# A chunked sigmoid recurrence: shorter warm-up, a different interleaving of four streams, and one operand added on TensorE for some steps

## The chip, the cores and the metric

The kernel runs on one core of one Trainium2 chip. The metric is the device time of one execution in microseconds, of which the median over the runs is taken. A separately profiled execution gives the trace that all views here are read from.

## The reference, cut to what matters

The input is 32 images of 128 channels and 64 x 64 pixels. Layer 0 adds a group norm followed by a dynamic 3 x 3 convolution. Layer 1 treats the 4096 pixels of an image as tokens of 128 channels and adds a windowed attention, and then this recurrence over the tokens, which is all that the change touches:

```python
Wx = jnp.einsum('bti,hi->bth', x, W)
flat = Wx.reshape(B * T, H)
mean = jnp.mean(flat, axis=0)
var = jnp.var(flat, axis=0)
Wx = ((flat - mean) * jax.lax.rsqrt(var + BN_EPS) * gamma + beta).reshape(B, T, H)
Vt = V.T

def step(yt, wx_t):
    yt = jax.nn.sigmoid(wx_t + yt @ Vt)
    return (yt, yt)
y0 = jnp.zeros((B, H), dtype=Wx.dtype)
_, ys = jax.lax.scan(step, y0, jnp.swapaxes(Wx, 0, 1))
```

Here B = 32 images, T = 4096 tokens, H = 128 channels. V is the orthogonal factor of a QR decomposition. The ys are added to the tokens. All data are float32.

## The kernel before

The first 4018 us work through the images: convolution, attention and the product with W. They leave the tokens plus attention in the output in HBM, and the raw products z in the HBM tensor `z_d`, one image after the other. The tile `frames` in SBUF, which the images use for their input, is filled with z of the first two images towards the end. Two vectors per channel, `scl` and `shf`, fold the batch norm, so that a step computes sigmoid(scl z + shf + V y).

Then `by_runs` does the recurrence. It cuts the 4096 tokens of an image into 128 chunks (`NRUN`) of 32 (`RUN`) and runs all chunks side by side, as columns of one matrix. A chunk doesn't know the state that enters it, so it starts `WARM` tokens earlier, in the chunk before, from a rough state; the map contracts, and after the warm-up the state is close enough. The first chunk starts from zero and stays out of the warm-up (127 of 128 columns). A bound on V computed at the start of the kernel (`okv`, the largest row sum of the absolute values of a product of V with itself) chooses between `by_runs` and `by_steps`, which walks over the 4096 tokens one after the other.

Two images form a group (`NI` = 2), so a step works on 128 partitions x 256 columns, and there are 16 groups. A step has four operations, one on each engine, and each waits for the one before:

- TensorE: the product of `fVT` with the state `yw` into a PSUM tile `v` (L1926 in the warm-up, L1932 after it). A float32 product is two MATMUL records in the trace.
- VectorE: v = scl z + v, with z read from the group's tile with a step of 32 floats (L1927, L1933).
- ScalarE: the state yw = sigmoid(v + shf) (L1928, L1936). The first step of a group has no product, and ScalarE reads z itself (L1923).
- GpSimd: outside the warm-up, the state is copied over z in the tile (L1937).

Two buffers of `yw` and two of `v` alternate in each stream. When a group is through, GpSimd issues two DMAs that add its tile onto the output in HBM (L1940; here called the hand-over of the group). Then `load` (L1903, on SP's queue) fetches group g + 6 into the tile that has come free, so it has to wait for those DMAs. There are five tiles `zr` and `frames`: six groups in SBUF.

Four streams (`NSTR`) overlap their chains: stream j does groups j, j + 4, j + 8 and j + 12. They are Python generators. The loop under `live` takes a step of each stream in turn, and lets a further one in every 13 steps (`lag`), until all four run. The schedule is manual: instructions stand in each engine's queue in the order in which the Python code emits them, and each engine works through its queue in that order.

Of the kernel before, what the change touches and what calls it, by code (L numbers as in the profile page):

```python
# [8 lines left out]
F32 = mybir.dt.float32  # L9
AF = mybir.ActivationFunctionType  # L10
ALU = mybir.AluOpType
AX = mybir.AxisListType

P = 128
# [17 lines left out]
NQ = 8  # L32
UNIT = 256
RUN = 32
WARM = 20
NRUN = T // RUN
NI = 2
NSTR = 4
# [20 lines left out]
class Clock:  # L59
# [88 lines left out]
    def take(self, eng, pool):  # L148
        t = min(pool, key=lambda t: self.after(eng, t, True))
        pool.remove(t)  # L150
        return t
# [106 lines left out]
def hybrid_kernel(  # L258
# [24 lines left out]
    nc = tc.nc  # L283
# [4 lines left out]
    of = out.rearrange("b c h w -> c b (h w)")  # L288
# [107 lines left out]
    with tc.tile_pool(name="sb2", bufs=1) as sb2, tc.tile_pool(  # L396
        name="ps2", bufs=1, space=bass.MemoryType.PSUM
    ) as ps2:
        vv = ps2.tile([P, P], F32, name="vv")
        nc.tensor.matmul(vv, fVT, fVT, start=True, stop=True)  # L400
        va_ = sb2.tile([P, P], F32, name="va_")
        nc.scalar.activation(va_, vv, AF.Abs)
        vr = sb2.tile([P, 1], F32, name="vr")
        nc.vector.tensor_reduce(vr, va_, axis=AX.X, op=ALU.add)
        vt_ = ps2.tile([P, P], F32, name="vt_")
        nc.tensor.transpose(vt_, vr.to_broadcast([P, P]), ident)
        vm = sb2.tile([P, 1], F32, name="vm")
        nc.vector.tensor_reduce(vm, vt_, axis=AX.X, op=ALU.max)
        nc.vector.tensor_scalar(vm, vm, 1.2, None, ALU.is_le)
        nc.vector.tensor_copy(okv, vm)  # L410
    contr = nc.values_load(okv[0:1, 0:1], min_val=0, max_val=1)

# [1470 lines left out]
    def by_runs():  # L1883
# [3 lines left out]
        with ExitStack() as pb:  # L1887
# [8 lines left out]
            def load(g):  # L1896
                if g < NG:
                    if g % (NSTR + 2):
                        zs[g] = zp.tile([P, NI, NRUN, RUN], F32, name="zr")
                    else:  # L1900
                        zs[g] = framed.rearrange("p i (c r) -> p i c r", r=RUN)
                    for i in range(NI if g else 0):
                        nc.sync.dma_start(  # L1903
                            zs[g][:, i].rearrange("p c r -> p (c r)"), z_d[g * NI + i]
                        )
# [1 line left out]
            for g in range(NSTR + 2):  # L1907
                load(g)

            def stream(j):  # L1910
                yw = []
                for i in range(2):
                    yw.append(hp.tile([P, NI, NRUN], F32, name=f"yw{j}_{i}"))
                    nc.vector.memset(yw[i], 0.0)
                for g in range(j, NG, NSTR):
                    zt = zs[g]
                    if g >= NSTR:
                        for i in range(2):
                            nc.vector.memset(yw[i][:, :, 0:1], 0.0)
                    for r in range(RUN - WARM, RUN):  # L1920
                        y, z = yw[r % 2][:, :, 1:], zt[:, :, 0 : NRUN - 1, r]
                        if r == RUN - WARM:
                            nc.scalar.activation(y, z, AF.Sigmoid, bias=shf, scale=scl)  # L1923
                        else:
                            ps = p_v.tile([P, NI, NRUN], F32, name=f"v{j}")[:, :, 1:]
                            nc.tensor.matmul(ps, fVT, yw[1 - r % 2][:, :, 1:], start=True, stop=True)  # L1926
                            nc.vector.scalar_tensor_tensor(ps, z, scl, ps, ALU.mult, ALU.add)  # L1927
                            nc.scalar.activation(y, ps, AF.Sigmoid, bias=shf)  # L1928
                        yield
                    for r in range(RUN):  # L1930
                        ps = p_v.tile([P, NI, NRUN], F32, name=f"v{j}")
                        nc.tensor.matmul(ps, fVT, yw[1 - r % 2], start=True, stop=True)  # L1932
                        nc.vector.scalar_tensor_tensor(  # L1933
                            ps, zt[:, :, :, r], scl, ps, ALU.mult, ALU.add
                        )
                        nc.scalar.activation(yw[r % 2], ps, AF.Sigmoid, bias=shf)  # L1936
                        nc.gpsimd.tensor_copy(zt[:, :, :, r], yw[r % 2])  # L1937
                        yield
                    for i in range(NI):
                        nc.gpsimd.dma_start(  # L1940
                            of[:, g * NI + i],
                            zt[:, i].rearrange("p c r -> p (c r)"),
                            accum_op=ALU.add,
                            max_dma_last_dim=8192,
                        )
                    load(g + NSTR + 2)

            live = [stream(j) for j in range(NSTR)]
            step = 0
            lag = (WARM + RUN) // NSTR  # L1950
            while live:
                for st in list(live[: 1 + step // lag] if step < lag * NSTR else live):
                    try:
                        next(st)
                    except StopIteration:
                        live.remove(st)
                step += 1

    def by_steps():

# [108 lines left out]
```

## Time and profile before

| what | value |
|---|---|
| median of 3 runs | 4610.49 us (4604.08 to 4615.4) |
| profiled execution, its own time | 4604.75 us |
| its span | 4602.9 us |
| VectorE busy in the whole span | 3577.4 us (78%) |
| first sigmoid of the recurrence | 4020.07 us |
| hand-over of group 0, 12, 15 | 4135.80, 4488.86, 4577.82 us |
| VectorE instructions L1927 and L1933 in the recurrence | 816 |
| ScalarE, first step of a group (L1923) | 0.815 us each |
| ScalarE, other steps (L1936) | 0.473 us each |
| GpSimd, copy (L1937) | 0.686 us mean, 0.629 median |

The span is the time from the first to the last event of the profiled execution; the execution's own time lies 1.85 us above it. Instructions of the recurrence carry their own line numbers, while those of the images nearly all have L242, since a helper records them. In the timeline, a group such as "MATMUL ... x2" is one product. What stands in brackets behind an instruction is the idle time of its engine before it, and what ended it. A DMA share above 1 means that the engines' packet times overlap a little: the 16 DMA engines are full.

### The profile page before, as it was taken

To read this page: it belongs to the slowest core of one execution; us is meant where nothing else is said; L and a number is where in the kernel's file an instruction comes from. 1 tells how busy PE (TensorE), PEld (TensorE's weight loads), DVE (VectorE), ACT (ScalarE), POOL (GpSimd) and SP (SyncE) were. 2 spreads that over 40 slices of the span, in tenths; PEclk is the share of its full clock that TensorE was granted. 3 is DMA by queue.
4 is the path that set the end of the run, shared out by engine and by line. 5 is a ranking of instruction groups with operands and counts; after the bars stand their busy time and mean duration, and the time that the engine had idled before them with its cause. 6 is when DMAs were issued, how large, how long until landed. Compare 5 with 4: busy or idle time off the path is not lost.

```text
span 4602.9 us, 102351 instructions
## 1 busy us (share of the span) xinstructions
PE 4175.5 (91%) x41527; PEld 2065.4 (45%) x41527; DVE 3577.4 (78%) x5421; ACT 2492.7 (54%) x4012; POOL 1650.6 (36%) x1652
## 2 busy tenths in 40 slices
PE   5999999899899999999999999999999987379995
PEld 2444444444444444444444444444444444135552
DVE  7778878787787787788687787888778754479994
ACT  1455555455555555555545555555555555258883
POOL 3333333333333333334232332333333321037764
PEclk9999999999999999999999999999999999689996
DMA  3435555454554555564555455555555454439997
GB/s 99 129 117 168 180 160 184 153 175 152 172 179 154 177 178 167 168 196 157 168 177 171 161 185 156 170 169 168 164 185 163 152 197 146 169 156 249 286 261 147
DMA packets 467575, 789.38 MB, mean 171 GB/s; under 512 B 338048, under 2 KB 348304, under 8 KB 434320
## 3 DMA queue, kind: packets, MB, share of 16 engines
q1 hardware_dynamic: 456480, 715.38, 47.1%
q0 software_dynamic: 8704, 67.11, 7.1%
q8 instruction: 332, 5.44, 0.5%
q14 instruction: 155, 1.27, 0.1%
q10 hardware_dynamic: 1904, 0.18, 0.0%
HBM read 499.06 MB, written 276.76 MB: 169 GB/s over the span
## 4 chain that ended last, share of the span: by engine, by line
PE 60%; DVE 20%; DMA 9%; ACT 4%; issue 4%; POOL 2%; SPq 1%; ACTq 0%; DVEq 0%; POOLq 0%
PE nm L242 35%; PE sc L242 14%; PE av L242 10%; DVE zt L242 4%; DVE v L1933 4%; DMA place<-r_d 3%; DVE v L1927 2%; ACT ex L242 2%; DVE frames L242 2%; DMA out_dram<-zr 2%; DVE u L242 1%; PE v L1932 1%; SPq L242 1%; DMA zr<-z_d 1%; DVE cp L242 1%
## 5 line engine op out<-in xcount | busy, mean ns | idle before, releaser
L242 ACT ACTIVATE ex<-sc 128x1152 f32<-128x1152 f32 x896 | 1012.5, 1130 | 838.7 <-PE sc L242 802.5
L242 POOL TENSOR_TENSOR qe<-qs,mqk 128x576 f32<-128x576 f32 x448 | 609.4, 1363 | 746.4 <-PE sc L242 741.0
L242 PE MATMUL nm<-u,w 128*128 128x512 f32 x1536 | 800.4, 633 | 15.9 <-POOL w L242 14.8
L242 PE MATMUL sc<-qe,ks 32*128 32x288 f32 x7168 | 698.7, 459 | 105.0 <-ACT ext L242 41.9
L242 PE MATMUL av<-ex,VE 128*32 128x144 f32 x14336 | 631.2, 294 | 21.5 <-DVE avs L242 21.3
L242 PEld LDWEIGHTS sc<-qe,ks 32*128 32x128 f32 x7168 | 285.6, 185 | 621.1 <-issue 181.5
L242 PEld LDWEIGHTS av<-ex,VE 128*32 128x32 f32 x14336 | 371.5, 110 | 350.0 <-issue 255.8
L242 POOL TENSOR_TENSOR u<-frames 128x528 f32<-128x528 f32 x256 | 380.3, 1493 | 186.8 <-PE nm L242 184.3
L242 PE MATMUL nm<-u,h 128*128 128x512 f32 x768 | 396.9, 625 | 3.6 <-DVE frames L242 3.6
L242 PEld LDWEIGHTS nm<-u,w 128*128 128x128 f32 x1536 | 258.6, 192 | 287.4 <-issue 257.0
L1932 PE MATMUL v<-yw,fVT 128*128 128x256 f32 x1024 | 323.7, 439 | 44.8 <-ACT yw L1936 43.7
L242 ACT ACTIVATE place<-zt 128x1024 f32<-128x1024 f32 x256 | 262.7, 1052 | 82.7 <-DVE zt L242 62.1
L1937 POOL COPY zr<-yw 128x256 f32<-128x256 f32 x416 | 257.2, 686 | 125.6 <-ACT yw L1936 125.6
L1936 ACT ACTIVATE yw<-v,shf 128x256 f32<-128x256 f32 x512 | 241.2, 473 | 107.6 <-DVE v L1933 71.4
L242 PE MATMUL nm<-zt,fWc 128*128 128x512 f32 x512 | 290.7, 665 | 6.9 <-ACT zt L242 6.9
L1933 DVE SCALAR_TENSOR_TENSOR v<-zr,scl,v 128x256 f32<-128x256 f32 x416 | 257.9, 668 | 42.0 <-PE v L1932 42.0
L242 DVE SCALAR_TENSOR_TENSOR u<-u,u 128x528 f32<-128x528 f32 x256 | 244.3, 967 | 46.4 <-POOL u L242 44.9
L242 ACT COPY zt<-nm 128x512 f32<-128x512 f32 x256 | 149.5, 585 | 206.7 <-PE nm L242 204.0
L242 PE MATMUL nm<-place,avg 128*32 128x256 f32 x3072 | 239.8, 394 | 13.0 <-ACT place L242 12.8
L1926 PE MATMUL v<-yw,fVT 128*128 128x254 f32 x608 | 206.0, 436 | 46.8 <-ACT yw L1923 27.6
L1932 PEld LDWEIGHTS v<-yw,fVT 128*128 128x128 f32 x1024 | 158.9, 193 | 195.7 <-ACT yw L1936 189.5
L242 DVE SCALAR_TENSOR_TENSOR zt<-sc,gbk,zt 128x576 f32<-128x576 f32 (+1 forms) x192 | 175.0, 912 | 74.1 <-PE sc L242 73.0
(204 smaller groups left out, 6595.0 us busy)
## 6 DMA issues: line engine op xcount, KB each, us to landing
place<-r_d SPq DMA_DIRECT2D x384, 512.0 KB
place<-in_conv_k_dram SPq DMA_DIRECT2D x128, 576.0 KB
x_d<-frames SPq DMA_DIRECT2D x32, 2112.0 KB
place<-x_d SPq DMA_DIRECT2D x128, 528.0 KB
frames<-in_x_dram SPq DMA_DIRECT2D x128, 512.0 KB
out_dram<-zt SPq DMA_DIRECT2D x64, 1024.0 KB
z_d<-zt SPq DMA_DIRECT2D x64, 1024.0 KB
zr<-z_d SPq DMA_DIRECT2D x26, 2048.0 KB
```

The source lines that it names most:

```text
L242: got = f(*args, **kw)
L1926: nc.tensor.matmul(ps, fVT, yw[1 - r % 2][:, :, 1:], start=True, stop=True)
L1927: nc.vector.scalar_tensor_tensor(ps, z, scl, ps, ALU.mult, ALU.add)
L1932: nc.tensor.matmul(ps, fVT, yw[1 - r % 2], start=True, stop=True)
L1933: nc.vector.scalar_tensor_tensor(ps, zt[:, :, :, r], scl, ps, ALU.mult, ALU.add)
L1936: nc.scalar.activation(yw[r % 2], ps, AF.Sigmoid, bias=shf)
L1937: nc.gpsimd.tensor_copy(zt[:, :, :, r], yw[r % 2])
```

## The change

There are three parts.

- `WARM` goes from 20 to 16, and the bound that chooses `by_runs` from 1.2 to 1.02.
- The round-robin of the generators is replaced by a list scheduler in Python. `Stream` holds where a stream stands (group `g`, step `k`, engine `phase`), `take` keeps for each engine when it will be free by assumed costs, and the loop emits the instruction that can start first. The product of step k of group g is given an earliest time, 90 + 26 (g - 4 left / 48), with `left` the steps still to do. This is an order and not a wait: nothing holds an instruction back on the chip but its operands and its queue.
- A step may be done without VectorE. `inject` emits ahead of the step's own product a product of the diagonal matrix `dg` = diag(scl) with z into the same PSUM tile, and the own product is accumulated onto it (`start=not whole`). ScalarE then reads the sum. This is allowed for group 0, and for other groups where at most two streams are left; the scheduler decides at which steps. `dg` is computed once by VectorE (L1911 of the changed kernel).

The emitted order has 752 products with `fVT`, 58 diagonal products (32 in group 0, 7 in group 14, 19 in group 15), 694 VectorE instructions, 768 sigmoids and 512 copies.

```diff
 NQ = 8
 UNIT = 256
 RUN = 32
-WARM = 20
+WARM = 16
 NRUN = T // RUN
 NI = 2
 NSTR = 4
@@ -406,7 +406,7 @@
         nc.tensor.transpose(vt_, vr.to_broadcast([P, P]), ident)
         vm = sb2.tile([P, 1], F32, name="vm")
         nc.vector.tensor_reduce(vm, vt_, axis=AX.X, op=ALU.max)
-        nc.vector.tensor_scalar(vm, vm, 1.2, None, ALU.is_le)
+        nc.vector.tensor_scalar(vm, vm, 1.02, None, ALU.is_le)
         nc.vector.tensor_copy(okv, vm)
     contr = nc.values_load(okv[0:1, 0:1], min_val=0, max_val=1)
 
@@ -1907,54 +1907,127 @@
             for g in range(NSTR + 2):
                 load(g)
 
-            def stream(j):
-                yw = []
-                for i in range(2):
-                    yw.append(hp.tile([P, NI, NRUN], F32, name=f"yw{j}_{i}"))
-                    nc.vector.memset(yw[i], 0.0)
-                for g in range(j, NG, NSTR):
-                    zt = zs[g]
-                    if g >= NSTR:
-                        for i in range(2):
-                            nc.vector.memset(yw[i][:, :, 0:1], 0.0)
-                    for r in range(RUN - WARM, RUN):
-                        y, z = yw[r % 2][:, :, 1:], zt[:, :, 0 : NRUN - 1, r]
-                        if r == RUN - WARM:
-                            nc.scalar.activation(y, z, AF.Sigmoid, bias=shf, scale=scl)
+            dg = hp.tile([P, P], F32, name="dg")
+            nc.vector.tensor_scalar_mul(dg, ident, scl)
+            DIAG, PE, DVE, ACT, POOL, LAT = 0.9, 0.43, 0.56, 0.46, 0.64, 0.2
+            free = {"PE": 0.0, "DVE": 0.0, "ACT": 0.0, "POOL": 0.0}
+
+            def take(eng, at, cost):
+                at = max(at, free[eng])
+                free[eng] = at + cost
+                return at + cost
+
+            class Stream:
+
+                def __init__(self, j):
+                    self.j, self.g, self.k, self.phase = j, j, 0, "ACT"
+                    self.at = 10.0 * j
+                    self.ahead = self.ps = None
+                    self.read, self.kept = [-9.0, -9.0], [-9.0, -9.0]
+                    self.yw = []
+                    for i in range(2):
+                        self.yw.append(hp.tile([P, NI, NRUN], F32, name=f"yw{j}_{i}"))
+                        nc.vector.memset(self.yw[i], 0.0)
+
+                def step(self, k):
+                    warm = k < WARM
+                    c = slice(1, NRUN) if warm else slice(0, NRUN)
+                    r = RUN - WARM + k if warm else k - WARM
+                    z = zs[self.g][:, :, 0 : NRUN - 1, r] if warm else zs[self.g][:, :, :, r]
+                    return c, r, z
+
+                def start(self):
+
+                    at = max(self.at, free[self.phase])
+                    if self.phase == "PE":
+                        left = WARM + RUN - self.k
+                        at = max(at, 90.0 + 26.0 * (self.g - left * NSTR / (WARM + RUN)))
+                    return at
+
+                def due(self):
+
+                    if self.phase == "PE":
+                        return self.start()
+                    if self.phase == "DVE":
+                        return max(self.at, free["DVE"]) + DVE + ACT + 2 * LAT
+                    return max(self.at, free["ACT"]) + ACT + LAT
+
+                def inject(self):
+
+                    k = self.k if self.phase == "PE" else self.k + 1
+                    c, r, z = self.step(k)
+                    self.ahead = p_v.tile([P, NI, NRUN], F32, name=f"v{self.j}")
+                    nc.tensor.matmul(self.ahead[:, :, c], dg, z, start=True, stop=False)
+                    take("PE", self.read[k % 2] + LAT, DIAG)
+
+                def go(self):
+
+                    k = self.k
+                    c, r, z = self.step(k)
+                    y = self.yw[r % 2]
+                    if self.phase == "PE":
+                        whole = self.ahead is not None
+                        self.ps = self.ahead if whole else p_v.tile([P, NI, NRUN], F32, name=f"v{self.j}")
+                        self.ahead = None
+                        nc.tensor.matmul(self.ps[:, :, c], fVT, self.yw[1 - r % 2][:, :, c], start=not whole, stop=True)
+                        self.at = take("PE", self.at, PE) + 0.38
+                        self.phase = "ACT" if whole else "DVE"
+                        return
+                    if self.phase == "DVE":
+                        v = self.ps[:, :, c]
+                        nc.vector.scalar_tensor_tensor(v, z, scl, v, ALU.mult, ALU.add)
+                        self.at = take("DVE", self.at, DVE) + 0.25
+                        self.phase = "ACT"
+                        return
+                    if k:
+                        nc.scalar.activation(y[:, :, c], self.ps[:, :, c], AF.Sigmoid, bias=shf)
+                    else:
+                        nc.scalar.activation(y[:, :, c], z, AF.Sigmoid, bias=shf, scale=scl)
+                    end = take("ACT", max(self.at, self.kept[k % 2] + LAT), ACT)
+                    self.read[k % 2] = end
+                    if k >= WARM:
+                        nc.gpsimd.tensor_copy(z, y)
+                        self.kept[k % 2] = take("POOL", end + LAT, POOL)
+                    self.at, self.phase, self.k = end + LAT, "PE", k + 1
+                    if self.k == WARM + RUN:
+                        g = self.g
+                        for i in range(NI):
+                            nc.gpsimd.dma_start(
+                                of[:, g * NI + i],
+                                zs[g][:, i].rearrange("p c r -> p (c r)"),
+                                accum_op=ALU.add,
+                                max_dma_last_dim=8192,
+                            )
+                        load(g + NSTR + 2)
+                        self.g, self.k, self.phase = g + NSTR, 0, "ACT"
+                        if self.g < NG:
+                            for i in range(2):
+                                nc.vector.memset(self.yw[i][:, :, 0:1], 0.0)
                         else:
-                            ps = p_v.tile([P, NI, NRUN], F32, name=f"v{j}")[:, :, 1:]
-                            nc.tensor.matmul(ps, fVT, yw[1 - r % 2][:, :, 1:], start=True, stop=True)
-                            nc.vector.scalar_tensor_tensor(ps, z, scl, ps, ALU.mult, ALU.add)
-                            nc.scalar.activation(y, ps, AF.Sigmoid, bias=shf)
-                        yield
-                    for r in range(RUN):
-                        ps = p_v.tile([P, NI, NRUN], F32, name=f"v{j}")
-                        nc.tensor.matmul(ps, fVT, yw[1 - r % 2], start=True, stop=True)
-                        nc.vector.scalar_tensor_tensor(
-                            ps, zt[:, :, :, r], scl, ps, ALU.mult, ALU.add
-                        )
-                        nc.scalar.activation(yw[r % 2], ps, AF.Sigmoid, bias=shf)
-                        nc.gpsimd.tensor_copy(zt[:, :, :, r], yw[r % 2])
-                        yield
-                    for i in range(NI):
-                        nc.gpsimd.dma_start(
-                            of[:, g * NI + i],
-                            zt[:, i].rearrange("p c r -> p (c r)"),
-                            accum_op=ALU.add,
-                            max_dma_last_dim=8192,
-                        )
-                    load(g + NSTR + 2)
-
-            live = [stream(j) for j in range(NSTR)]
-            step = 0
-            lag = (WARM + RUN) // NSTR
+                            live.remove(self)
+
+            live = [Stream(j) for j in range(min(NSTR, NG))]
             while live:
-                for st in list(live[: 1 + step // lag] if step < lag * NSTR else live):
-                    try:
-                        next(st)
-                    except StopIteration:
-                        live.remove(st)
-                step += 1
+                best = None
+                for st in list(live):
+                    at = st.start()
+                    if best is None or (at, st.g) < best[0]:
+                        best = (at, st.g), st, False
+                    k = st.k if st.phase == "PE" else st.k + 1
+                    if st.ahead is not None or k >= WARM + RUN or (st.g and len(live) > 2):
+                        continue
+                    at = max(free["PE"], st.read[k % 2] + LAT, st.at if st.k == 0 else 0.0)
+                    if st.phase != "PE" and at + DIAG > st.due():
+                        continue
+                    if any(o is not st and at + DIAG > o.due() + 0.1 for o in live):
+                        continue
+                    if (at, st.g) < best[0]:
+                        best = (at, st.g), st, True
+                _, st, ahead = best
+                if ahead:
+                    st.inject()
+                else:
+                    st.go()
 
     def by_steps():
 
```

## Prediction

> **What bounds the kernel now.** The stage tables come first, because the page averages two very different programs: the images, to about 4018 us, and the recurrence, which alone is changed. I cut its last 580 us where the number of live streams changes. After the stretch and its length come busy us (and counts) of PE, PEld, DVE, ACT, POOL, then the clock of TensorE, the DMA share and GB/s.
>
> ```profile
> 4022.00:4052.00 30.00, 14.72 (x25) 6.01 (x24) 7.94 (x13) 5.66 (x12) 0.00 (x0) 0.50 1.01 428
> ...
> 4200.00:4230.00 30.00, 29.48 (x106) 15.83 (x106) 29.83 (x55) 25.33 (x54) 21.35 (x35) 1.00 0.97 230
> ...
> 4440.00:4470.00 30.00, 29.27 (x106) 15.92 (x106) 29.65 (x55) 25.32 (x54) 21.64 (x37) 1.00 1.02 278
> ...
> 4530.00:4560.00 30.00, 17.73 (x37) 8.18 (x36) 11.55 (x18) 8.52 (x18) 13.94 (x21) 0.61 0.74 150
> 4560.00:4603.00 43.00, 7.75 (x14) 2.99 (x12) 4.53 (x7) 3.31 (x7) 6.74 (x9) 0.50 0.64 130
> ```
>
> There are three regimes. With one stream (first and last rows) nothing is busy, TensorE has half its clock, and a step is pure latency. With four streams VectorE is full, and so, from 4200 on, are the DMA engines. Next, the timeline gives one stream's chain at full clock:
>
> ```profile
> 4068.15 0.70 PE L1932 MATMUL v<-yw,fVT 128*128 128x256 f32 x2 [0.64 <-ACT yw L1936]
> ...
> 4068.89 0.66 DVE L1933 SCALAR_TENSOR_TENSOR v<-frames,scl,v 128x256 f32<-128x256 f32 x1 [0.69 <-PE v L1932]
> ...
> 4069.59 0.47 ACT L1936 ACTIVATE yw<-v,shf 128x256 f32<-128x256 f32 x1 [0.88 <-DVE v L1933]
> ...
> 4070.11 0.70 PE L1932 MATMUL v<-yw,fVT 128*128 128x256 f32 x2 [0.65 <-ACT yw L1936]
> ```
>
> From product to eviction 0.74, to sigmoid 0.70, to the next product 0.52: 1.96 us a step. Alone, at half clock, it is 2.53 (4569.32 to 4571.85). The chain of waits in order of time says what ends last when all streams run:
>
> ```profile
> 4123.91 1.76 DVE v L1933 x3
> ...
> 4253.12 35.16 DMA out_dram<-zr
> 4288.77 24.66 DMA zr<-z_d
> ...
> 4331.51 1.69 DVE v L1933 x3
> ```
>
> Three evictions in 1.69, so 0.563 each and 2.25 for a round of four; and twice the chain runs through a group's hand-over (write, then the load into its place). The waits of the DMA queues and of the engines in this stage:
>
> ```profile
> SPq L1903 <- DMA out_dram<-zr: 230.2, 8, 32.4
> ...
> ACT yw L1923 <- DMA zr<-z_d: 2.8, 3, 1.5
> ```
>
> Loads always wait for a write, yet cost the engines only 2.8 us: the DMA is full, but just in time. Hand-overs in the timeline come 29.4 us apart (4135.8 for group 0 to 4488.9 for group 12: 353.1 for twelve), as do the DMA's completions (a write issued to its queue at 4370.69, the following load at 4406.35, the one after at 4435.78). So two limits coincide at 29.4.
>
> **What the Trainium skill says.** "TensorE: Matmul & The Clock Gate", Part 1, has half clock when idle and full clock after about 3.4 us of sustained work; the trace agrees in kind (0.50 with one stream, 1.00 with four), though products became short only 7.4 us after the second stream began (4053.0 to 4060.4). The same page, "Architectural detail", says ScalarE's queue is strict first-in, first-out: a sigmoid that waits for a load holds up all streams. "SBUF — State Buffer", "Door 1: The DMA port swizzle", says that reads pay when each access crosses a 16-byte line; the new product reads every 32nd float. ScalarE shows such a price (0.815 us at L1923, reading z, against 0.473 reading PSUM); no TensorE row does. "DMA: Bandwidth & Descriptors", "SWDGE vs HWDGE vs iDMA", says that a DMA engine takes the two kinds of queue in turn. The trace agrees: a load of 4.2 MB beside a write takes 24.66, against some 9.9 alone (the ten first DMAs, 21 MB in about 49 us).
>
> **The change, part by part.**
>
> *Fewer steps.* 4 warm-up steps less in 16 groups: 64 products, evictions and sigmoids. 64 x 0.563 = 36 us of VectorE, on the path wherever four streams run. The bound 1.02 only chooses the branch: V is orthogonal, so the row sums of |V V^T| should lie close to 1, and the same branch runs. Cost nil.
>
> *Diagonal products.* The order of instructions has 58 (32 in group 0, 26 in groups 14 and 15), so 694 evictions are left of 816. Each takes the 0.66 us eviction off its stream's chain (0.74 + 0.52 = 1.26 left) and puts d on TensorE. Ordinary products queued behind each other start 0.43 apart (two passes, 0.215 each, in the trace). Low end d = 0.43, if stride is free; high end two passes of 256 at ScalarE's strided 0.815/256, 1.6. VectorE's 0.563 per 256 strided elements gives two passes of 0.5; the diff's own scheduler has 0.9. I take d = 1.0. A lone step is then 0.43 + 1.0 = 1.43, and TensorE is full, so the clock should come up.
>
> *Start.* The order gives group 0 ten lone steps, 12 rounds with group 1, 12 with 1 and 2 (11 with a diagonal product), 13 with all. Lone: first sigmoid 0.9, 7.4 us cold (3.4 steps at about 2.2), 6.6 x 1.43: 17.7. Two streams: the other stream's chain, 2.0 x 12 = 24.0 (TensorE needs 1.86). Three: 3 x 0.43 + 1.0 = 2.29, x 11, and one of 2.02: 27.2. Four: 13 x 2.25 = 29.3. Last eviction to hand-over 2. Sum 100.2. The first sigmoid moves by 0.3 (dg, on VectorE's queue ahead of the memsets; the 2.2 us of memsets, all issued at once, lie ahead of no eviction for ten steps) to 4020.4. **First hand-over 4120.6**, against 4135.8. Groups 1 to 3 need their loads, which landed by 4029.7, 4039.5 and 4049.3; their first sigmoids come at about 4032, 4042 and 4053, so no wait, but little slack.
>
> *Four streams.* From hand-over 0 to 12 the order has 564 evictions: x 0.563 = 317.5 us, against 353.1: 26.5 a group. That is what VectorE wants; the DMA gives a group per 29.4. Count from hand-over 0. Its write lands at about 28 (with half of the next load beside it, as at 4164.4), the next at 52 without the idle gap of before, then one per 29.4; each load lands 25 after the write before it. Loads of groups 7 to 15 land at 77, 106, 136, 165, 195, 224, 253, 283, 312. The order wants them after 221, 279, 319, 365, 409, 467, 507, 553 and 597 evictions less the 91 made: 73, 106, 128, 154, 179, 212, 234, 260, 285. The wait of each first sigmoid stops all streams, so delays add: 4, 0, 4, 3, 5, 0, 4, 3, 5, **27 us of new waiting** on loads at the first sigmoid of a group. So group 15 starts at 312 and hand-over 12 comes at 345. The VectorE time saved here is mostly given back to the DMA. GpSimd's and SP's queues keep their content: 512 copies of about 0.63 and 16 hand-overs of 2.44 to issue, as before, and 26 loads in the same order, so I count nothing for them; GpSimd has 21 of 30 us filled.
>
> *End.* Three streams: 10.5 rounds x 2.02 (4506.01 to 4508.04) = 21.2. Two with diagonal products: three rounds hold 6 products and 4 diagonal ones, 6.58, so 11.5 x 2.19 = 25.2, against 28.9 for 13 rounds at a sinking clock. Lone: 11 x 1.43 + 1.5 = 17.2 against 33.3. Hand-over 15 at 408.6. Its write took 25.1 to the end of the span (4577.82 to 4602.9), and here the write of group 14 (issued 391.5, landing about 413) is still ahead of it: 413 + 20 + 3 = 436. **End 4120.6 + 436 = 4556.6, 46.3 less than the span of 4602.9.** That execution took 4604.75, the median of the three shown is 4610.49; 4610.49 x 4556.6 / 4602.9 = 4564.
>
> **Rivals.** *Loads in time.* If the loads slip in without a wait and d = 0.43, the start is 95 us, hand-over 15 comes at 374, and the bare DMA sum ends it: 10 x 29.4 + 6 x 20 + 4 = 418 after 4115.4, so 4533, or 4541 as a median. For it: before, the waits were 2.8 us. Against: a DMA share of 1.02 leaves no reserve.
>
> *The diagonal product is dear.* Everything counts d twice: at d = 1.6 start 117.5 and hand-over 15 at 424.6, end 4588 (4596). At 2.0 start 130, hand-over 15 at 435, end 4611. Break-even is near 1.9; at 2.4 the kernel is **slower**, about 4642. It needs over four times an ordinary product, past the high end above; the half clock holding on would be the way there.
>
> *It does something else.* If the tight bound failed, `by_steps` would run 4096 dependent steps; at an estimated 0.6 us (sigmoid and product shorter than the 1.26 above) 2460 us in place of 580.
>
> **How the numbers follow.** Loads bind, d about 1: 0.64, 4564. Loads in time: 0.17, 4541. d of 1.3 to 1.75, still faster: 0.10, about 4585. d near 1.9, within 0.3%, about what a measurement here can tell from no change: 0.03. Slower by d: 0.05; by the branch: 0.01. Hence 0.91, 0.03, 0.06. The range goes from the DMA floor with 3 us to spare, 4538, to d = 1.6, 4596.
>
> **What would show it.** Right: hand-over 0 near 4121; waits of the first sigmoid on loads of some 25 us in place of 2.8; VectorE below 9.5 tenths in the four-stream stretches; hand-overs 29.4 apart still; clock 1.00 to the last step; diagonal products starting about 1.0 ahead of the next product. Wrong: hand-overs 26.5 apart and no load waits (then the DMA had reserve), a lone step over 2 us (d or the clock), or a write of group 15 that starts at once.

## The result, and the profile after

The changed kernel takes **4564.54 us** (median; 4559.51 to 4565.91), the kernel before took 4610.49 us on the same chip. The ratio is **0.9899 [0.9885, 0.9914]**: 46 us or 1.0% faster. The forecast was 4564. The sum came out right although some of its terms did not; the ledger shows where they cancel. All stages are counted from the first sigmoid, since the end of the images stage, which neither kernel changes, wanders by some 10 us either way between executions (4013 to 4034 us in the profiles below).

| stage, us | before | predicted | after |
|---|---|---|---|
| first sigmoid | 4020.07 | 4020.4 | 4022.85 |
| from there to hand-over 0 | 115.7 | 100.2 | 95.3 |
| hand-over 0 to 12 | 353.1 | 345 | 357.3 |
| gaps 12 to 13, 14, 15 | 26.8, 28.8, 33.3 | 21.2, 25.2, 17.2 | 20.9, 22.5, 16.5 |
| hand-over 15 to the end of the span | 25.1 | 27.4 | 28.9 |
| span | 4602.9 | 4556.6 | 4564.1 |

The span fell by 38.8: the start gave 20.4, the last three gaps gave 29.2; the middle **cost** 4.2 although it has four steps less in every group, the tail cost 3.8, and the images ended 2.8 later. (The profiled execution took 4565.91.)

The stage table of the kernel after answers to the one of before. The columns are the stretch and its length, then busy us (and counts) of PE, PEld, DVE, ACT, POOL, the clock of TensorE, the DMA share and GB/s.

```profile
4024.00:4054.00 30.00, 29.37 (x86) 16.96 (x87) 5.24 (x8) 13.98 (x28) 1.14 (x2) 0.90 1.00 427
4118.00:4142.00 24.00, 23.61 (x83) 12.19 (x83) 23.32 (x45) 20.18 (x43) 20.00 (x33) 1.00 0.95 214
4142.00:4168.00 26.00, 25.52 (x91) 13.39 (x91) 25.32 (x48) 22.02 (x47) 18.64 (x31) 1.00 1.03 266
4194.00:4234.00 40.00, 34.72 (x117) 19.73 (x116) 33.66 (x61) 28.67 (x60) 25.33 (x42) 0.91 0.97 260
4284.00:4318.00 34.00, 26.80 (x89) 15.56 (x88) 25.54 (x47) 21.33 (x45) 20.41 (x33) 0.85 1.03 288
4496.00:4519.00 23.00, 23.00 (x77) 14.84 (x77) 4.59 (x7) 10.92 (x23) 16.12 (x27) 1.00 0.97 195
4519.00:4535.00 16.00, 13.65 (x41) 6.59 (x39) 0.00 (x0) 5.22 (x11) 9.60 (x14) 1.00 0.94 188
4118.00:4475.00 357.00, 327.38 (x1128) 177.95 (x1127) 322.78 (x589) 274.23 (x576) 252.41 (x408) 0.95 0.97 259
```

Read the first row and the two from 4496 on: with one or two streams TensorE is now busy 85 to 100% of the time at a clock of 0.90 to 1.00; before, the clock was 0.50 with one stream. The rows from 4118 and 4142 (gaps of 23.3 and 26.6) show what VectorE alone would allow: it is busy 97% of the time. In the gaps from 4194 and from 4284 it is busy 84% and 75%. The last row is the whole middle: VectorE has 322.78 us of work in 357, the clock is 0.95. The same row of the kernel before, in the same columns, has VectorE at 98%, full clock and full DMA:

```profile
4136.00:4489.00 353.00, 342.83 (x1226) 184.12 (x1226) 347.33 (x635) 295.53 (x624) 249.92 (x409) 1.00 0.99 262
```

So 25 us of VectorE work did leave the middle, and all of it came back as idle time. The waits of the kernel after in the recurrence name the first part of it (the line reads: engine, tile and line that waited, what it waited for; us in total, times, longest). One of the six, of 0.97 us, lies ahead of hand-over 0:

```profile
ACT yw L1985 <- DMA zr<-z_d: 24.4, 6, 7.7
```

ScalarE's first sigmoid of a group waits 24.4 us for loads, against 2.8 before. The chain in order of time (start, length, what) now passes three times through a load, and what follows the load is TensorE's line and not VectorE's:

```profile
4172.70 25.16 DMA zr<-z_d
4197.97 0.82 ACT yw L1985
4198.84 6.67 PE v L1972 x18
4205.54 27.33 PE v L1972 x96
...
4257.77 36.52 DMA out_dram<-zr
4294.78 23.85 DMA zr<-z_d
4318.74 0.82 ACT yw L1985
...
4377.82 38.26 DMA out_dram<-zr
4416.58 24.11 DMA zr<-z_d
4440.80 0.82 ACT yw L1985
```

The timeline around the first of these shows why TensorE comes next (start, length, instruction, idle time before it and what ended that):

```profile
4197.97 0.81 ACT L1985 ACTIVATE yw<-zr,shf,scl 128x254 f32<-128x254 f32 x1 [4.63 <-DMA zr<-z_d]
...
4200.09 0.66 DVE L1978 SCALAR_TENSOR_TENSOR v<-zr,scl,v 128x254 f32<-128x254 f32 x1 [4.80 <-PE v L1972]
...
4200.94 0.66 DVE L1978 SCALAR_TENSOR_TENSOR v<-zr,scl,v 128x256 f32<-128x256 f32 x1 [0.20 <-PE v L1972]
...
4201.80 0.66 DVE L1978 SCALAR_TENSOR_TENSOR v<-zr,scl,v 128x256 f32<-128x256 f32 x1 [0.19 <-PE v L1972]
```

After a wait of 4.63 us the evictions start 0.85 apart and no longer 0.563, each behind a product: the granted clock of TensorE is 0.50 there, and 1.00 again only from 4204.0 on. That is the second part of the lost time.

### The profile page after: what moved, and what is told of

It is laid out like the page before. It is cut to its first block, busy times and chain, and to the rows that moved or that the text cites. A ratio compares the mean times of both kernels' runs of the same rounds, so it can differ in the third digit from the quotient of the medians.

```text
span 4564.1 us, 102113 instructions
## 1 busy us (share of the span) xinstructions
PE 4165.5 (91%) x41515; PEld 2074.1 (45%) x41515; DVE 3511.6 (77%) x5300; ACT 2465.8 (54%) x3948; POOL 1648.9 (36%) x1652
## 3 DMA queue, kind: packets, MB, share of 16 engines
q14 instruction: 153, 1.25, 0.1%
## 5 line engine op out<-in xcount | busy, mean ns | idle before, releaser
L242 PEld LDWEIGHTS av<-ex,VE 128*32 128x32 f32 x14336 | 371.7, 110 | 349.7 <-issue 255.6
L1972 PE MATMUL v<-yw,fVT 128*128 128x254 f32 (+1 forms) x1504 | 436.9, 428 | 34.8 <-ACT yw L1985 25.0
L1983 ACT ACTIVATE yw<-v,shf 128x254 f32<-128x254 f32 (+1 forms) x752 | 354.6, 474 | 120.6 <-DVE v L1978 48.3
L1978 DVE SCALAR_TENSOR_TENSOR v<-zr,scl,v 128x256 f32<-128x256 f32 (+1 forms) x585 | 347.2, 665 | 90.3 <-PE v L1972 89.8
L1972 PEld LDWEIGHTS v<-yw,fVT 128*128 128x128 f32 x1504 | 241.7, 194 | 243.6 <-ACT yw L1983 194.1
L242 POOL TENSOR_TENSOR kt<-ks,mqk 128x384 f32<-128x384 f32 (+1 forms) x96 | 78.3, 815 | 426.2 <-ACT ks L242 381.4
```

Of the source, the lines that this page charges most:

```text
L242: got = f(*args, **kw)
L1972: nc.tensor.matmul(self.ps[:, :, c], fVT, self.yw[1 - r % 2][:, :, c], start=not whole, stop=True)
L1978: nc.vector.scalar_tensor_tensor(v, z, scl, v, ALU.mult, ALU.add)
L1983: nc.scalar.activation(y[:, :, c], self.ps[:, :, c], AF.Sigmoid, bias=shf)
```

## The experiments

Ratios are to the kernel before on the same chip, with 95% intervals; the medians come from several chips, so kernels are compared by their ratios. The other columns come from one profile of each kernel, in us: the stages as in the ledger, the time from the first sigmoid to the end of the span, and the waits of first sigmoids for loads into `zr`. The time to the end leaves out the wandering of the images stage: in the two kernels that were profiled twice it differs by 0.8 (after, after_again) and 0.4 (after_same, same_again).

| kernel | median | ratio | to hand-over 0 | 0 to 12 | first sigmoid to end | load waits |
|---|---|---|---|---|---|---|
| before | 4610.49 | 1 | 115.7 | 353.1 | 582.8 | 2.8 |
| after | 4564.54 | 0.9899 [0.9885, 0.9914] | 95.3 | 357.3 | 541.3 | 24.4 |
| warm_only | 4589.81 | 0.9954 [0.9938, 0.9969] | 106.1 | 347.4 | 559.3 | 18.3 |
| no_diag | 4596.19 | 0.9965 [0.9951, 0.9979] | 105.0 | 368.8 | 566.4 | 31.0 |
| warm20 | 4593.63 | 0.9963 [0.9950, 0.9977] | 104.4 | 375.9 | 569.1 | 20.5 |
| dg_twice | 4607.51 | 0.9992 [0.9982, 1.0002] | 117.6 | 358.8 | 581.9 | 25.7 |
| after_half | 4542.15 | 0.9841 [0.9824, 0.9858] | 95.5 | 328.1 | 512.4 | 1.2 |
| before_half | 4605.59 | 0.9991 [0.9982, 1.0000] | 117.5 | 349.4 | 581.8 | none |
| plain | 4520.46 | 0.9809 [0.9795, 0.9822] | 95.4 | 328.1 | 498.2 | 2.2 |
| even | 4565.25 | 0.9907 [0.9891, 0.9924] | 93.7 | 349.7 | 535.4 | 15.5 |
| after_same | 4553.66 | 0.9877 [0.9860, 0.9894] | 95.5 | 344.8 | 529.1 | 14.3 |
| even_same | 4554.95 | 0.9882 [0.9866, 0.9899] | 93.9 | 339.9 | 526.3 | 6.6 |
| after_again | 4574.08 | 0.9914 [0.9897, 0.9930] | 95.3 | 356.2 | 540.4 | 24.8 |
| same_again | 4561.29 | 0.9885 [0.9866, 0.9904] | 95.6 | 344.4 | 528.6 | 13.3 |

In no_diag and even_same one first sigmoid waits for a load into `frames` as well, 4.2 and 1.7.

The theory behind the forecast: the ends gain by fewer and shorter steps, and the middle is held by the DMA. The first four runs below take the change apart, the next three take load off the DMA, the last five ask what could be had back.

### warm_only: the kernel before with the shorter warm-up alone

```diff
-WARM = 20
+WARM = 16
-        nc.vector.tensor_scalar(vm, vm, 1.2, None, ALU.is_le)
+        nc.vector.tensor_scalar(vm, vm, 1.02, None, ALU.is_le)
```

> The kernel before with 16 warm-up steps and the bound 1.02, round-robin as it was. Theory (from hand-over 0 on, the DMA engines set the pace, about 29.4 us a group while writes and loads run together): hand-over 0 some 9 us earlier, hand-over 0 to 12 about 350 us in place of 353, since the 27 us of VectorE saved there turn into waits of first sigmoids for loads; the last three hand-overs about 7 us earlier. Total about 19 us less than before (ratio 0.996). Rival (VectorE alone sets the pace of four streams): hand-over 0 to 12 in 326 us, total about 43 us less (0.991).

The ratio is 0.9954, 21 us: close to the theory's 0.996, and not the rival's 0.991. The start is 9.6 shorter (four lone steps), the middle only 5.7, though 48 evictions have left it (27 us of VectorE). The new wait stands in its list of waits:

```profile
ACT yw L1923 <- DMA zr<-z_d: 18.3, 6, 7.1
```

So the time saved in the middle turns into waiting for loads with the old order too; it is not something that the new scheduler brings.

### no_diag: the change without the diagonal products

```diff
-                    if st.ahead is not None or k >= WARM + RUN or (st.g and len(live) > 2):
+                    if True:
                         continue
```

> The changed kernel with no diagonal product allowed, so that all 752 products have their eviction on VectorE. Theory (the diagonal product shortens single-stream steps and keeps the TensorE clock up at both ends): hand-over 0 about 14 us later than in the changed kernel, the two last hand-over gaps longer by 4 and 14 us, hand-over 0 to 12 the same 357; total about 30 us more than the changed kernel, near 0.9965 of before. Rival (the scheduler's order brings the gain and the diagonal product is hidden): within 8 us of the changed kernel, 0.990 to 0.992.

The total is as expected (0.9965), and so are the last two gaps (4.0 and 13.0 longer than in after). But hand-over 0 comes 9.7 later and not 14, and the middle is not the same: the scheduler emits another order, in which hand-overs come 13 to 50 apart and up to 74 evictions lie ahead of one, so it grows to 368.8. Its stage table, in the same columns, has half clock at both ends (the first stretch begins before the first sigmoid, at 4032.89):

```profile
4020.00:4053.00 33.00, 11.74 (x22) 5.69 (x22) 14.74 (x35) 7.36 (x13) 0.00 (x0) 0.50 0.79 324
4540.00:4575.00 35.00, 16.76 (x29) 7.00 (x28) 9.72 (x15) 7.56 (x16) 13.09 (x19) 0.50 0.83 172
```

In the first 30 us of the recurrence (from 1 us after the first sigmoid) the clock is 0.68 without the diagonal products and 0.90 with them, and in the last gap 0.50 and 1.00: they bring it up. What they are worth as a whole, 30 us by the two ratios, also holds the change of order: of 25.2 from the first sigmoid to the end, 11.6 lie in the middle.

### dg_twice: every diagonal product issued twice

```diff
+                    nc.tensor.matmul(self.ahead[:, :, c], dg, z, start=True, stop=True)
                     nc.tensor.matmul(self.ahead[:, :, c], dg, z, start=True, stop=False)
```

> The changed kernel with each diagonal product issued twice into the same tile, the second time from a fresh start, so that d is 1.72 in place of the 0.86 that the trace shows between a diagonal product and the next product. Theory (every diagonal product lies on the path, the break-even of the prediction is near 1.9): a lone step about 2.15 in place of 1.29, hand-over 0 about 25 us later, the last two gaps about 14 and 9 us longer, total about 46 us more than the changed kernel, 0.998 to 1.002 of before. Rival (a part of the diagonal products hides behind the sigmoid): less than 30 us more, under 0.9965.

Its timeline has a lone step of 2.14 in place of 1.29, read from product to product:

```profile
4034.01 0.61 PE L1973 MATMUL v<-yw,fVT 128*128 128x254 f32 x2
...
4036.15 0.61 PE L1973 MATMUL v<-yw,fVT 128*128 128x254 f32 x2
```

Doubling takes d from 0.86 to 1.72, hand-over 0 comes 22.3 later, the last two gaps are 11.9 and 8.8 longer, and the whole gain is gone (0.9992, 4607.51). So every diagonal product lies on the path, as the forecast priced it. Break-even lies a little above 1.72 and below the forecast's 1.9, in line with a middle that is 14 longer than it assumed.

### warm20: the change with the old warm-up

```diff
-WARM = 16
+WARM = 20
```

> The changed kernel with WARM back at 20 (the bound stays 1.02): scheduler and diagonal products without the shorter warm-up. The order then has 612 evictions between hand-overs 0 and 12 in place of 564, in gaps of 40, 46, 44 and 74, and 107 before hand-over 0 in place of 91. Theory (the middle is set by the DMA at about 29.4 us a group, so 48 evictions more there cost little): hand-over 0 about 9 us later, hand-over 0 to 12 about 360 in place of 357, the last three gaps as in the changed kernel, total about 13 us more than the changed kernel (0.993 of before). Rival (VectorE sets the pace, and the shorter warm-up is worth its 64 evictions): 36 us more or over, 0.998.

0.9963 lies between the two values named. The last three gaps are the same to 0.1 us (20.9, 22.5, 16.5): they contain no warm-up step. The start is 9.1 longer. The middle was mispredicted: 375.9 in place of 360.

```profile
4130.00:4506.00 376.00, 351.56 (x1225) 188.29 (x1225) 348.81 (x636) 296.89 (x625) 253.09 (x408) 0.97 0.93 246
```

The DMA share of 0.93 suggests why: this order leaves 48 to 50 us ahead of every fourth hand-over, in which the queue of writes can run empty. VectorE's work sets a lower bound for the middle, the order decides how far above it the middle lies. In this kernel the four warm-up steps are worth 29 us by the ratios, against 21 in the kernel before. Scheduler and diagonal products without the shorter warm-up bring 17 (4610.17 to 4593.63), so the parts alone make 38 of the 46. Counted from the first sigmoid to the end they make 37.2 of 41.6 (23.5 and 13.7). That some gain exists only together is not shown: the difference is within the intervals.

### after_half and before_half: half of each later load

```diff
+                    if g >= NSTR + 2:
+                        zs[g] = zs[g - NSTR - 2]
-                    if g % (NSTR + 2):
+                    elif g % (NSTR + 2):
...
+                        n = T // 2 if g >= NSTR + 2 else T
                         nc.sync.dma_start(
-                            zs[g][:, i].rearrange("p c r -> p (c r)"), z_d[g * NI + i]
+                            zs[g][:, i].rearrange("p c r -> p (c r)")[:, 0:n], z_d[g * NI + i][:, 0:n]
```

> The changed kernel with the loads of groups 6 to 15 halved: only the first 2048 tokens of an image are loaded, the rest of the tile keeps what stood there, and a tile is reused image by image as the frames tile is. Theory (the DMA limits the middle): waits of first sigmoids for loads near 0 in place of 24, TensorE clock 1.00 throughout, hand-over 0 to 12 in about 322 us in place of 357, total about 36 us less than the changed kernel (0.982 of before). Rival (the emitted order and refilling after a group change cost the 357 us, not the loads): hand-over 0 to 12 above 345, total at most 10 us less.

> The kernel before with the same halved loads. Theory (before, VectorE and DMA limits coincided at 29.3 and 29.4 us a group): at most 8 us less than before (0.998 to 1.000), hand-over 0 to 12 at about 346 in place of 353. Rival (before was bound by the DMA with VectorE well below it): 20 us less or more (under 0.996).

Before stands almost where it was (0.9991); after gains 27 us by the ratios (0.9841 against 0.9899), less than the 36 expected. The edit also lets a load wait for its own image's write alone, which by itself shortens the middle by 12.5 (after_same below); plain, without that part, takes the middle to the same length. The stretch between its hand-overs and its waits:

```profile
4116.00:4438.00 322.00, 316.41 (x1107) 164.68 (x1108) 313.99 (x578) 270.60 (x566) 246.35 (x401) 1.00 0.96 221
```

```profile
ACT yw L1988 <- DMA zr<-z_d: 1.2, 1, 1.2
```

With the loads cheap, VectorE is busy 97.5%, the clock is 1.00 and the middle takes 328.1. Together with plain this separates the two: before is held by VectorE with the DMA just keeping up, after is held by the DMA. It also measures the middle almost without waits, which the forecast had as 564 x 0.563 = 317.5.

### plain: the hand-over as a plain write

```diff
-                                accum_op=ALU.add,
```

> The changed kernel with the hand-over as a plain write: the DMA puts the states into the output and does not add them to what stands there, so the addition is left out. The bytes of the tile stay the same. Theory (the accumulating write takes about 20 us of the 16 DMA engines per group, twice what a load of the same bytes takes, and the DMA limits the middle): a write alone about 10 us, waits of first sigmoids near 0, hand-over 0 to 12 about 328 as with halved loads, the last hand-over followed by about 17 us in place of 29; total about 40 us less than the changed kernel (0.981 of before). Rival (only the loads matter, the writes run in the shadow): hand-over 0 to 12 still over 345, total under 20 us less.

The kernel leaves out the addition onto the output. 0.9809, as expected. The middle is 328.1, the same as with half loads by an entirely different relief, and the end comes 15.9 after the last hand-over in place of 28.9. Stage table and issue table (the last column is the median us from issue to landing; 25.1 in the kernel after):

```profile
4120.00:4450.00 330.00, 324.45 (x1136) 168.88 (x1136) 321.93 (x592) 276.95 (x580) 243.50 (x411) 1.00 0.70 280
```

```profile
out_dram<-zr POOLq DMA_DIRECT2D x26, 2048.0 KB, 10.0
```

The DMA share falls from 0.97 to 0.70. The page's line of the queue that carries the hand-overs (packets, MB, share of 16 engines over the span) has the price, first in the kernel after, then here:

```profile
q0 software_dynamic: 8704, 67.11, 7.2%
q0 software_dynamic: 8704, 67.11, 3.6%
```

7.2% of 4564 is 329 us, 20.5 a group; 3.6% of 4526 is 163, 10.2 a group. The addition in the write, and not its bytes, is what fills the DMA.

### even: the scheduler's costs set to those of the trace

```diff
-            DIAG, PE, DVE, ACT, POOL, LAT = 0.9, 0.43, 0.56, 0.46, 0.64, 0.2
+            DIAG, PE, DVE, ACT, POOL, LAT = 0.86, 0.43, 0.56, 0.46, 0.64, 0.06
-                        self.at = take("PE", self.at, PE) + 0.38
+                        self.at = take("PE", self.at, PE) + 0.31
-                        self.at = take("DVE", self.at, DVE) + 0.25
+                        self.at = take("DVE", self.at, DVE) + 0.09
```

> The changed kernel with the scheduler's assumed costs set to what the trace shows: diagonal product 0.86 in place of 0.9, 0.31 from product to eviction (0.38), 0.09 from eviction to sigmoid (0.25), 0.06 for the other hand-offs (0.2). The emitted order then has 45 to 49 evictions between hand-overs 0 to 12 in place of 40, 46, 44, 58, and 62 diagonal products. Theory (waits come where the order asks for a load before the DMA can give it, and its queue runs dry where the order leaves 58 evictions): hand-over 0 some 4 us earlier, hand-over 0 to 12 about 345 us in place of 357, total about 13 us less than the changed kernel (0.987 of before). Rival (the DMA sum fixes the end whatever the order): within 4 us of the changed kernel, 0.989 to 0.991.

The edit does what it says to the order: 45 to 49 evictions between hand-overs, where after has 40, 46, 44 and 58 in turn. The middle shrinks by 7.6 and the waits to 15.5 (longest 4.8). But the ratio is 0.9907 against 0.9899, no difference within the intervals; the expected 0.987 was missed. In this profile the last hand-over comes at 507.9 after the first sigmoid, against 512.4 in after, and the end at 535.4 against 541.3: the new order takes back 4.7 in the last three gaps (64.5 in place of 59.8). A gain of some 6 us is too small for the ratios to show.

### after_same: a load waits only for its own image's write

```diff
-                    if g % (NSTR + 2):
+                    if g >= NSTR + 2:
+                        zs[g] = zs[g - NSTR - 2]
+                    elif g % (NSTR + 2):
                         zs[g] = zp.tile([P, NI, NRUN, RUN], F32, name="zr")
```

> The changed kernel with each group's tile taken over from group g - 6 as the same tile, so that the load of an image waits for the write of that image alone, not for both writes of the group. The bytes stay. Theory (what is short is the time from hand-over to landed load, and the DMA serves both queues in turn, so a load that starts some 10 us earlier takes its share from a write that nobody waits for): waits of first sigmoids about 17 us in place of 24, hand-over 0 to 12 about 348 in place of 357, total about 8 us less than the changed kernel (0.988 of before). Rival (the DMA sum alone counts): no change, 0.990.

In the kernel after, a new tile is asked of the pool, and both of its loads wait for both writes of the group that held it. Here the group takes over the same tile, and each image's load waits for that image's write alone. SP's queue shows it: its loads wait 8 times for the writes of `zr` tiles in after, up to 32.6 us, and 16 times here, up to 15.1. Expected 0.988, measured 0.9877.

```profile
4129.00:4474.00 345.00, 326.92 (x1130) 176.67 (x1128) 323.03 (x588) 274.86 (x577) 252.53 (x409) 0.97 1.00 268
```

```profile
ACT yw L1987 <- DMA zr<-z_d: 14.3, 7, 4.1
```

The DMA share is 1.00, the waits are shorter by 10, none is over 4.1, and the middle is 12.5 shorter.

### even_same: both

> Both of the above. Theory: the gains add in part; hand-over 0 to 12 about 337, total about 20 us less than the changed kernel (0.9855 of before). Rival (the DMA sum alone counts): within 5 us of the changed kernel.

0.9882 against 0.9877: no gain over after_same alone, and the 0.9855 expected was missed. The waits are nearly gone (6.6), the middle is the shortest with full loads and adding writes (339.9), and still the end comes only 2.8 earlier than in after_same, 526.3 after the first sigmoid:

```profile
4120.00:4500.00 380.00, 359.70 (x1260) 193.45 (x1260) 349.70 (x633) 298.34 (x632) 285.28 (x463) 0.99 1.01 263
```

The start is 1.7 shorter than in after_same and the middle 4.9, but the last three gaps are 4.8 longer (64.6 against 59.8). And a DMA share of 1.01 over 380 us leaves little to reorder. From hand-over 0 to the end this kernel takes 432.4 us; an estimate of the DMA work in it, 16 writes of 20.5 (the price in plain's section) and ten loads of some 9.8 (the first ten DMAs of the kernel before moved 21 MB in about 49 us), is 426. So the sum of DMA work is nearly the bound here, and only less or cheaper DMA work would move the end far, as plain did.

### after_again and same_again: the better version, side by side

> The changed kernel once more, beside the next one on the same chip: 0.990 of before.

> The changed kernel with loads released image by image, once more beside it, to see whether it is the better of the two. Theory (a load that starts earlier takes its share from a write that nobody waits for): 0.988 of before, some 8 us under the changed kernel. Rival (the DMA sum alone counts, and the earlier result was chance): no difference, 0.990.

On one chip the medians are 4574.08 (4565.34 to 4577.60) and 4561.29 (4558.49 to 4565.21): after_same is 12.8 us better than the kernel after, the two ranges just failing to overlap, and 51 us better than the kernel before. Middle and waits repeat (356.2 and 24.8 against 344.4 and 13.3), and so does the time from the first sigmoid to the end (540.4 against 528.6). It is the version to keep.

## Why the prediction was right, and where only its sum was

**What bounds what: right.** VectorE and the DMA coincided at 29.4 us a group before; with VectorE's part cut, the DMA held the middle. Half loads freed it (after_half) and so did plain writes (plain), while half loads did almost nothing for the kernel before.

**The diagonal product: right in kind, d too dear.** d was taken as 1.0 and measures 0.86. The timeline of a lone step, start and length first:

```profile
4032.12 0.61 PE L1972 MATMUL v<-yw,fVT 128*128 128x254 f32 x2
...
4032.57 1.02 PE L1960 MATMUL v<-frames,dg 128*128 128x254 f32 x2
4032.77 0.47 ACT L1983 ACTIVATE yw<-v,shf 128x254 f32<-128x254 f32 x1 [0.81 <-PE v L1972]
...
4033.41 0.61 PE L1972 MATMUL v<-yw,fVT 128*128 128x254 f32 x2
```

From product to product 1.29; the diagonal product takes 0.84 of it (4032.57 to 4033.41), and the sigmoid ends inside it, so that the step is TensorE's two products and nothing else, about 0.43 + 0.86. The forecast had the form right and 1.43 as the size.

**The start: 4.9 too long.** With 1.29 a lone step, 1.945 for a round of two streams (2.0 assumed), 2.15 for one of three (by d; 2.29 assumed) and cold steps of 1.78 (2.2 assumed), the sum falls by some 4; that accounts for nearly all of it.

**The middle: 12.8 too short, by three terms.** The forecast was 317.5 + 27 = 344.5 (rounded to 345 in the ledger, hence 12.3 there); it took 357.3.

- 564 evictions x 0.563 is not the time of the stretch without waits. That is 328.1 (after_half, plain): 10.6 more. In after_half the gaps with 40, 44, 46 and 58 evictions all lie 0.8 to 1.0 above evictions x 0.563, so it is a fixed cost of each of the 12 changes of group, in which a stream has a first sigmoid of 0.82 and no eviction.
- The waits were 23.4 in this stretch, not 27; five in place of seven, of up to 7.7.
- The clock was not in the sum. It was put at nothing (the forecast had 1.00 to the last step), and 5.8 us are left for it: 357.3 less 328.1 is 29.2, of which 23.4 are the waits.

Where the 5.8 lie can be read by laying the gaps of after beside those of after_half, which has the same order. Seven of the twelve agree within 0.1 us. The other five are the ones with a wait, and the only ones in which the granted clock falls:

| gap up to hand-over | wait | longer than in after_half | of it beyond the wait | clock at 0.50, us from the span's start |
|---|---|---|---|---|
| 4 | 4.63 | 6.2 | 1.6 | 4197.2 to 4204.0 |
| 7 | 6.69 | 8.4 | 1.7 | 4285.9 to 4296.2 |
| 8 | 1.48 | 2.3 | 0.8 | 4320.1 to 4323.5 |
| 11 | 7.75 | 8.8 | 1.0 | 4405.4 to 4415.6 |
| 12 | 2.90 | 3.5 | 0.6 | 4442.9 to 4446.3 |

In the first of them the slow products account for the rest: the first eviction starts 1.25 after its product (4198.84 to 4200.09) where 0.74 is usual, and four intervals of 0.85 in place of 0.563 follow, 1.7 in all. No run isolates the clock, and even the wait of 1.48 was followed by half clock.

The DMA ends 29.4 apart were also only an average: this order leaves 40 us ahead of hand-over 4, with 58 evictions. The load that had waited for the write of group 3 was issued at 4231.43 and the next write only at 4233.71; the DMA share was 0.22 and 0.00 in the two us from 4230 to 4232. The share of 0.97 in the place of 0.99 probably stands for this gap and its like.

**The end: 3.8 too long, and right in its steps.** 59.8 for the last three gaps against 63.6, by d; and the write of group 15 does wait behind that of group 14, with 28.9 to the end where 27.4 were forecast.

**The sum.** Start −4.9, middle +12.3, last gaps −3.8, tail +1.5, first sigmoid +2.4: 7.5 over the forecast span of 4556.6, as measured. In the medians even that is gone: the forecast came from span to median by adding 7.4, as it stood for the kernel before (4610.49 to 4602.9), while here the profiled execution (span 4564.1, time 4565.91) is the longest of its runs, and the median only 0.4 above its span. From the first sigmoid to the end the forecast was 536.2 and the measurement 541.3. A forecast within 1 us is luck; the ledger says that its steps are good to about 5 us, and the middle to 12.

**The rivals.** Loads in time fell with the 24.4 us of waits. The dear diagonal product fell with 0.86; dg_twice shows that twice that d takes the whole gain. The kernel did what it says: there are no 4096 dependent steps.

## What to carry to other kernels

Where two resources coincide at the same period, price a cut of one against the other: in the middle 25 us of VectorE work went and no time with it, while the latency-bound ends, where nothing was full, gave all of the gain. Give such ends work for an idle engine, if it shortens the chain and keeps that engine's clock up. And when buffers come free by DMA, let each load wait for just the write that it overwrites: three lines were worth another 13 us here.

## What the runs showed of the hardware

- A float32 product whose moving operand is read with a step of 128 bytes takes 0.86 us for 256 columns, twice the 0.43 of a dense one. No run reads z densely, so that the step is the cause is inferred: the other operand is a 128 x 128 tile in both. The Trainium skill ("SBUF — State Buffer", "Door 1: The DMA port swizzle") led to expect a price for reads that go to another 16-byte line at each access; here it is a factor of 2.0, for TensorE.
- A write that adds takes the DMA engines 20.5 us for 4.2 MB, a plain write of the same packets 10.2.
- The clock of TensorE fell to half in or just after waits of 1.48 to 7.75 us, and stayed there for 6.8, 10.2, 3.4, 10.2 and 3.4 us. From the restart of TensorE to full clock it took up to 5.2 us (4198.84 to 4204.0), at the start of the recurrence 6.2 (4023.7 to 4029.9). The Trainium skill ("TensorE: Matmul & The Clock Gate", Part 1) has the work judged in free-running windows of about 3.4 us; the five stretches are multiples of that, and one window of work was not always enough.
- GpSimd's issue of a hand-over, 2.44 us, holds up the copies behind it: right after 4518.79 a lone sigmoid started 2.15 us after the end of the one before it, having waited for a copy to free its buffer; the others start 0.85 after, having waited for their products. In plain, whose issue takes 1.43, it was 1.15, and the last gap was 1.0 shorter.
